# A four-layer graph network on one core: loading scalars and biases first, and choosing which degree sums block 0 leaves to layer 1

## The chip, the core and the metric

The kernel runs on one core of a Trainium2 chip. Its engines work side by side, each through its own queue in order: TensorE (PE: matmuls; its weight loads are shown as PEld), VectorE (DVE), ScalarE (ACT), GpSimd (POOL), and SyncE (SP), which here only issues loads and stores. The metric is device time in microseconds (us), lower is better; the median of several runs is given.

## What is computed

Four layers follow each other on 4096 nodes with 64 features and one dense 4096 x 4096 adjacency matrix `adj` (64 MiB in float32). Each layer normalizes x, applies a ReLU, mixes rows through `adj` in its own way, and adds the result to x:

```python
h = relu(layernorm(x)); x = x + relu((adj @ h) @ W0.T + b0)            # layer 0
h = relu(layernorm(x))                                                 # layer 1
#   h, q, k by "lorentz_linear" with scale, scale_q, scale_k
#   att = adj * sigmoid((2 + 2 * qm @ k.T) / att_scale + att_bias);  x += normalized(att @ h)
h = relu(layernorm(x))                                                 # layer 2
#   deg = adj.sum(axis=1); w = adj / deg; weights from distances; x += expmap(...)
h = relu(layernorm(x))                                                 # layer 3
#   ranks of the nonzero entries of each row; x += (mask * 2**-(k - pos)) @ (h @ W3) + b3
```

The row sums of `adj` (`deg`, the degrees) are needed in layer 2 only. They can be collected whenever a piece of `adj` is in the core's memory, in layer 0 or in layer 1.

## The kernel before

**Tiling.** The rows of the result are cut into 8 blocks of 512 (`NB`, index `ib`). For one block, `adj` is read transposed in 16 groups (`NG`, index `g`), each a tile of 128 partitions x 2 x 512 float32 (512 KB), by one load on SP's queue (`feed`, line 837). Layers 0, 1 and 3 read all 128 groups each; ten buffers hold the groups in the first two layers (two pools of 6 and 4), so a load needs the buffer of the group ten places earlier.

**Start.** SP loads x in four quarters (line 175) and then the groups. For each quarter, `before0` computes the layernorm: two VectorE operations, a square on ACT (`qT<-HL` in the profile), a sum and a scaling on VectorE, a power on GpSimd (`lo_n`), and a VectorE operation that writes `HA`, the operand of the matmuls. Four times this makes `HA` complete. Layer 0's groups are multiplied as soon as `HA`'s quarter and the group are there (`l0_sums`, tiles `acc<-adj,HA`).

**After a block of layer 0** its result goes through a tail of small steps (`after0`, `before1`): ACT copies the accumulator (`e`), VectorE folds the block's degree tile (`dg<-dg`, 128x512), PE makes four matmuls with `W0T` and four with the degree tile (`tr<-W0T,e`, `tr<-ones_f,dg`), VectorE copies `deg` and adds the bias and the residual (`h<-tr,lines`, `x<-h,x`), then the next layernorm, a transposition, a matmul with `W1T`, ACT's chain of small operations (a table load for the sigmoid among them), VectorE's `lo_n`, GpSimd's power, `HL`, its transposition, a matmul with `WqkT`, and so on to q and k.

**Degree sums.** `group` decides for every group in which layer it is added to the degree tile. Blocks 1 to 6 leave the groups of `LEFT` to layer 1, block 0 leaves those of `FRONT`, block 7 leaves none. So in block 0, twelve groups are summed on VectorE in layer 0 (`dg<-adj`, a copy, for the first, then `dg<-dg,adj`), and the four of `FRONT` in layer 1. A group that is summed keeps its buffer until both its matmul and its sum are done.

**Scalars and biases.** Five scalars and two biases (`b0`, `b3`) are loaded into one row `line` (1 x 133). A matmul with a row of ones spreads it over 128 partitions, and a copy from PSUM makes `lines`, from which `scal`, `b0` and `b3` are read. Before the change, these loads are the first seven of a list of fifteen that ACT issues in `constants`, one after another; the eight after them are weights (`W0T` twice, `W1T`, its bias, and the q and k weights and biases). The last group of block 0 may be multiplied only when `lines` is planned (`None if d["last"] and "lines" not in opened`).

**The order.** The program is written out by a planner, `in_turn`. It holds one generator per strand of work; each yields an engine and an earliest time, and the strand that can start first by the planner's own costs (class `Pace`) is recorded next. Each engine then executes in exactly that order. A changed cost or a changed strand early on therefore moves operations in all engines' orders for as long as the strands of layers 0 and 1 are mixed. The order is fixed when the program is built: on the chip an operation whose operand is late holds up everything behind it on its engine. While PE is planned to wait, `keep_warm` adds filler matmuls.

**DMA semaphores.** The loads of SP and ACT report their landing through eight semaphores, dealt out in turn over both queues in the program's order. A load whose semaphore is still in use by an earlier load waits for that one to land before it is issued, and holds up what is behind it in its queue.

In the profile nearly all operations show line 139, that of the recording helper, so they are told apart by their tiles.

Of the kernel before, what the change touches and what calls it, by code (L numbers as in the profile page):

```python
# [19 lines left out]
D = 64  # L20
# [6 lines left out]
NG = NC // G  # L27
HALVED = 2
LEFT = (3, 7, 11, 15)
FRONT = (4,5,6,7,)  # L30
LAST = 2
WAIT = 0.6
EARLY = 12
# [113 lines left out]
def kernel(ctx: ExitStack, tc: tile.TileContext, a: dict, out: bass.AP):  # L147
# [3 lines left out]
    nc = tc.nc  # L151
    pace = Pace()
    PE, DVE, ACT, POOL = (
        InOrder(tc, e, pace, name)
        for e, name in (
            (nc.tensor, "PE"), (nc.vector, "DVE"), (nc.scalar, "ACT"), (nc.gpsimd, "POOL"),
        )
    )
# [23 lines left out]
    def fetch(t, src, to=loads):  # L182
        to.append(lambda: ACT.dma_start(out=t, in_=src))
# [9 lines left out]
    NS = len(SCALARS)  # L193
    line = const.tile([1, NS + 2 * D], F32, name="line")
    for n, name in enumerate(SCALARS):
        fetch(line[:, n : n + 1], a[name])
    for n, name in enumerate(("b0", "b3")):
        fetch(line[:, NS + n * D : NS + (n + 1) * D], a[name].rearrange("d o -> o d"))
    ones_row = const.tile([1, P], F32, name="ones_row")
    DVE.memset(ones_row, 1.0)  # L200
    lines = const.tile([P, NS + 2 * D], F32, name="lines")
# [58 lines left out]
    def later_constants():  # L260


        def patterns():
            yield "POOL", lambda: 60.0
            for t, one in [(t, 1.0) for t in rbs] + [(t, 0.25) for t in lbs]:
                POOL.memset(t, 0.0)
                for k in (1, 3):
                    POOL.memset(t[:, :, k, 1:2], one)

        def weights_of_ranks():  # L270


            yield "DVE", lambda: 150.0
            near_f = st["rows"].tile([P, P], F32, name="near_f", bufs=1)
            make_lower_triangular(nc, near_f, val=-1.0, diag=False)
            for q in range(4):
                b = slice(q * Q, (q + 1) * Q)
                DVE.tensor_copy(far[b, :], near_f[b, b])
            diag_f = st["rows"].tile([P, P], F32, name="diag_f", bufs=1)
            DVE.tensor_scalar(diag_f, ident, HERE, None, ALU.mult)  # L280
            yield "DVE", lambda: 150.0
            DVE.tensor_add(near_f, near_f, diag_f)
            DVE.tensor_copy(near, near_f)


            yield "DVE", lambda: 150.0
            DVE.memset(pick, 0.0)
            DVE.memset(spread, 0.0)
            for k in range(KH):
                DVE.memset(pick[:, k, k : k + 1], 1.0)  # L290
            for r in range(4):
                yield "DVE", lambda: 150.0
                b = slice(r * Q, (r + 1) * Q)
                for h in range(2):
                    to = spread[b, h, :, h * NC // 2 : (h + 1) * NC // 2]
                    DVE.tensor_copy(
                        to.rearrange("p q (k r) -> p q k r", r=4)[:, :, :, r],
                        ident[b, r * Q : r * Q + KH].unsqueeze(1).to_broadcast([Q, 4, KH]),
                    )

        return patterns(), weights_of_ranks()
# [48 lines left out]
    spare = [0, 1]  # L350

    def bank():
        k = spare.pop(0)
        t = (ps_two if k else ps_tr).tile([P, W], F32, tag=f"tr{k}", name="tr")
        in_use.append((t, k))
        return t

    def emptied(t):
        k = [k for k in in_use if k[0] is t][0]
        in_use.remove(k)  # L360
        spare.append(k[1])
# [219 lines left out]
    def after0(ib, acc, st):  # L581
        e = rows.tile([P, W], F32, tag="e", name="e")
        ACT.copy(e, acc)
        st["acc_free"][ib % 2] = pace.latest
        yield ON_V, lambda: st["dg_done"].get((0, ib))
        dg = st["dg"][0, ib]
        DVE.tensor_add(dg[:, 0, :], dg[:, 0, :], dg[:, 1, :])
        yield TURN

        ps = bank()  # L590
        v, n = ps[:, 0 : CB * D].rearrange("p (c k) -> p c k", k=D), CB * D
        for c in range(CB):
            b = slice(c * P, (c + 1) * P)
            PE.matmul(v[:, c, :], e[:, b], W0T, start=True, stop=True)
            PE.matmul(ps[:, n + c : n + c + 1], dg[:, 0, b], ones_f, start=True, stop=True)
        st["dg_free"][ib % 2] = pace.latest
        yield ON_V
        DVE.tensor_copy(deg[:, cs(ib), :], ps[:, n : n + CB].unsqueeze(2))
        s = rt("h", [P, CB, D])
        DVE.tensor_add(s, v, b0.to_broadcast([P, CB, D]))  # L600
        DVE.scalar_tensor_tensor(
            x[:, cs(ib), :], s, 0.0, x[:, cs(ib), :], ALU.max, ALU.add
        )
        yield ON_V
# [121 lines left out]
    def follow(gen, on=ON_V, evicts=False):  # L726

        tail.append(
            {"gen": gen, "on": on, "at": pace.latest, "slot": None, "evicts": evicts, "need": None}
        )  # L730
# [24 lines left out]
    def latest(*times):  # L755
        return None if None in times else max(times)
# [56 lines left out]
    opened = {}  # L813

    def with_mark(layer, ib, *gens):
        for gen in gens:
            yield from gen
        rows_at[layer, ib] = pace.latest
# [21 lines left out]
    def used(d):  # L840
        d["left"], d["at"] = d["left"] - 1, max(d["at"], pace.latest)

    def ready(t, more=0.0):
        return pace.ready[pace.name(t)] + more

    def arrival(d, more=0.0):
        return ready(d["adj"], more) if "adj" in d else None
# [43 lines left out]
    def group(layer, ib, g):  # L891
        degree = (g in (LEFT if ib else FRONT) and ib < NB - 1) == (layer == 1)
        return {"layer": layer, "ib": ib, "g": g, "degree": degree, "left": 1 + degree, "at": 0.0}
# [3 lines left out]
    l0 = [group(0, ib, g) for ib in range(NB) for g in range(NG)]  # L897
    l1 = [group(1, ib, g) for ib in range(2) for g in range(BEHIND)]
# [5 lines left out]
    for d in l0 + l1:  # L904
        n = done[d["layer"], d["ib"]] = done.get((d["layer"], d["ib"]), 0) + 1
# [19 lines left out]
    def degree_sums(layer, work):  # L925

        dg = st["dg"]
        for d in work:
            if not d["degree"]:
                continue  # L930
            first = (layer, d["ib"]) not in dg
            yield "DVE", lambda: latest(
                arrival(d, 4.0), st["dg_free"][d["ib"] % 2] if first else 0.0
            )
            if first:
                t = w01.tile([P, G, W], F32, tag="dg", name="dg", bufs=2)
                dg[layer, d["ib"]] = t
                st["dg_free"][d["ib"] % 2] = None
                DVE.tensor_copy(t, d["adj"])
            else:  # L940
                t = dg[layer, d["ib"]]
                DVE.tensor_add(t, t, d["adj"])
            used(d)
            if d is [e for e in work if e["degree"] and e["ib"] == d["ib"]][-1]:
                st["dg_done"][layer, d["ib"]] = pace.latest
# [5 lines left out]
    def l0_sums():  # L951
        for d in l0:
# [6 lines left out]
            if d["last"]:  # L959
                ib = d["ib"]  # L960
                follow(with_mark(1, ib, after0(ib, acc, st), before1(ib, st)), ON_S, evicts=True)

    def constants():
        for k in range(len(loads)):
            yield "ACT", lambda: 18.0 + 0.5 * k
            loads.pop(0)()
        yield "PE", lambda: 28.0 if spare else None
        ps = bank()
        PE.matmul(ps[:, 0 : NS + 2 * D], ones_row, line, start=True, stop=True)
        yield "DVE", lambda: ready(ps)  # L970
        DVE.tensor_copy(lines, ps[:, 0 : NS + 2 * D])
        emptied(ps)
        opened["lines"] = pace.latest
        yield "ACT", lambda: 32.0

        ACT.activation(es, scal[:, 0:3], AF.Exp)

        DVE.reciprocal(att_a, scal[:, 4:5])
        DVE.tensor_scalar(att_a, att_a, 2.0, None, ALU.mult)
        DVE.tensor_add(att_b, att_a, scal[:, 3:4])  # L980
        for k in range(len(later_loads)):
            yield "ACT", lambda: 240.0 + 0.5 * k
            later_loads.pop(0)()
# [146 lines left out]
    def l2_clamps():  # L1130
        for d in work:
            yield "POOL", lambda: d.get("square")
            v = part(d, d["v"]) if not d["shared"] else d["v"].rearrange("p c i -> p (c i)")[:, CLAMPED:]
            POOL.tensor_scalar(v, v, FLOOR, None, ALU.max)
            d["clamped"] = pace.latest
# [390 lines left out]
    def l3_sum():  # L1526
# [33 lines left out]
            (l2_coshs(), 0, once), (l2_clamps_v(), -1, once), (l2_weights2(), 1, lambda d: 2 if d["two"] else 1 if d["first"] else 0),  # L1560
        ),
        l2_clamps(), l2_gathers(), l3_weights(), l3_pass(), l3_masks(), l3_bias(),
        degree_sums(0, l0), degree_sums(1, l1), constants(), *later_constants(),
    ])


# [43 lines left out]
```

## Time and profile before

| | |
|---|---|
| median of 3 runs | 1097.06 us (1095.85 to 1101.96) |
| the profiled execution | 1101.81 us, of which the profile's span is 1100.1 us |
| busy, share of the span | PE 95%, DVE 85%, ACT 72%, PEld 42%, POOL 24% |
| moved by DMA | 271.77 MB, mean 247 GB/s |

How to read it: the span runs from the first to the last instruction of the profiled execution. A timeline line gives start, length, engine, source line, operation, out<-in, shape and count, and in brackets the idle time of the engine just before it with what ended it. Lines of the same kind that follow closely are merged, and the length is that of all of them. [...] In a table by stage, the clock and the loads' rate stand at the end of each line.

### The profile page before, as it was taken

Reading aid. Unit: us, or ns where it says so; the run is one execution under the profiler, and the core shown is the slowest. Engines: PE = TensorE matmul, PEld = TensorE weight load, DVE = VectorE, ACT = ScalarE, POOL = GpSimd, SP = SyncE. Lnnn points to the kernel's source line nnn. Section 1 sums busy time; section 2 is a strip of 40 time slices with the busy share of each in tenths; the row PEclk is TensorE's granted clock in tenths of the full one; section 3 lists DMA queues with packets and bytes.
Section 4 is the critical chain, followed back from the end, with each engine's and each line's share of the span. In section 5 each row is a group of like instructions: output and inputs, shape, how many; then the busy total and the mean of one; then the engine's idle time right before and its main releaser. Section 6 shows DMA issues by size and latency. Waiting matters only on the chain.

```text
span 1100.1 us, 16913 instructions
## 1 busy us (share of the span) xinstructions
PE 1043.9 (95%) x6030; PEld 466.8 (42%) x6030; DVE 931.7 (85%) x1526; ACT 788.1 (72%) x1224; POOL 261.0 (24%) x151
## 2 busy tenths in 40 slices
PE   7899999899999999999999999999999988999998
PEld 3344444333233333354544444445454443444444
DVE  7678999888999999888989998989899998666551
ACT  1144545476777777799989879888898866677776
POOL 3022312110110011243334334344444420000000
PEclk9989999999999999999999999999999998999999
DMA  8999999866687777544543543544545539899950
GB/s 309 406 346 389 381 389 382 306 227 217 212 277 265 241 262 271 177 143 167 192 173 125 192 181 118 190 151 155 171 156 189 190 128 398 346 409 408 411 225 10
DMA packets 76202, 271.77 MB, mean 247 GB/s; under 512 B 9046, under 2 KB 10070, under 8 KB 76118
## 3 DMA queue, kind: packets, MB, share of 16 engines
q1 hardware_dynamic: 75456, 270.57, 67.3%
q8 instruction: 47, 0.77, 0.3%
q14 instruction: 37, 0.30, 0.1%
q10 hardware_dynamic: 662, 0.13, 0.1%
HBM read 269.62 MB, written 1.05 MB: 246 GB/s over the span
## 4 chain that ended last, share of the span: by engine, by line
PE 54%; DVE 22%; issue 7%; ACT 6%; POOL 5%; DMA 3%; SPq 0%; ACTq 0%; POOLq 0%; DVEq 0%
PE acc L139 27%; PE mm L139 17%; PE tr L139 10%; DVE dg L139 5%; POOL v L139 5%; DVE t L139 3%; DVE w L139 3%; DVE sig L139 3%; DMA adj<-in_adjT_dram 3%; ACT sig L139 2%; ACT t L139 1%; ACT v L139 1%; DVE x L139 1%; DVE h L139 1%; ACT lo_sq L139 1%
## 5 line engine op out<-in xcount | busy, mean ns | idle before, releaser
L139 PE MATMUL acc<-w,HA 128*65 128x256 f32 (+1 forms) x736 | 246.2, 469 | 9.1 <-DVE w L139 8.9
L139 POOL TENSOR_SCALAR v<-v 128x1024 f32<-128x1024 f32 (+1 forms) x72 | 173.0, 2402 | 251.6 <-ACT v L139 248.9
L139 ACT ACTIVATE sig<-mm,att_b,att_a 128x1024 f32<-128x1024 f32 x128 | 150.8, 1203 | 58.0 <-PE mm L139 54.0
L139 ACT ACTIVATE wt<-mm,down 128x1024 fp32r<-128x1024 f32 x128 | 136.1, 1111 | 47.1 <-PE mm L139 44.7
L139 DVE TENSOR_TENSOR sig<-sig,adj 128x1024 f32<-128x1024 f32 x128 | 152.6, 1220 | 12.3 <-ACT sig L139 12.1
L139 DVE TENSOR_TENSOR dg<-dg,adj 128x1024 f32<-128x1024 f32 x113 | 137.9, 1221 | 1.6
L139 PE MATMUL mm<-qT,kT 64*64 64x512 f32 (+1 forms) x896 | 130.2, 599 | 6.6 <-ACT sig L139 6.1
L139 PEld LDWEIGHTS acc<-w,HA 128*65 128x65 f32 x736 | 94.3, 138 | 92.5 <-issue 50.2
L139 PE MATMUL acc<-sig,HL 64*64 64x512 f32 (+1 forms) x896 | 131.7, 603 | 1.4 <-DVE sig L139 1.4
L139 PE MATMUL acc<-adj,HA 128*64 128x512 f32 x512 | 125.6, 624 | 5.7 <-DMA adj<-in_adjT_dram 5.6
L139 ACT ACTIVATE v<-v,minus 128x1024 f32<-128x1024 f32 x72 | 79.1, 1098 | 27.5 <-POOL v L139 26.1
L139 DVE SCALAR_TENSOR_TENSOR t<-mm,t 128x1024 f32<-128x1024 f32 x72 | 83.6, 1160 | 14.9 <-PE mm L139 11.0
L139 DVE SCALAR_TENSOR_TENSOR t<-t,v 128x1024 f32<-128x1024 f32 x72 | 83.3, 1157 | 3.5 <-ACT t L139 2.9
L139 DVE TENSOR_TENSOR w<-t,adj 128x1024 f32<-128x1024 f32 x72 | 83.6, 1161 | 1.4
L139 DVE TENSOR_TENSOR w<-tr,adj 128x512 f32<-128x512 f32 x120 | 77.5, 683 | 7.4 <-PE tr L139 7.2
L139 ACT ACTIVATE t<-t 128x1024 f32<-128x1024 f32 x72 | 72.2, 1003 | 14.1 <-DVE t L139 14.0
L139 ACT ACTIVATE v<-mm 128x1024 f32<-128x1024 f32 x72 | 69.6, 967 | 13.7 <-PE mm L139 13.7
L139 PE MATMUL mm<-RT,LT 64*128 64x512 f32 (+1 forms) x288 | 78.0, 618 | 0.0
L139 PE MATMUL acc<-wt,S 128*128 128x512 f32 x256 | 76.2, 424 | 0.6 <-ACT wt L139 0.4
L139 ACT ACTIVATE t<-v 128x1024 f32<-128x1024 f32 x72 | 72.7, 1010 | 2.1
L139 ACT ACTIVATE v<-v 128x1024 f32<-128x1024 f32 x72 | 72.1, 1002 | 0.0
L139 PEld LDWEIGHTS mm<-qT,kT 64*64 64x64 f32 (+1 forms) x896 | 37.8, 140 | 77.9 <-ACT sig L139 35.4
(217 smaller groups left out, 1380.2 us busy)
## 6 DMA issues: line engine op xcount, KB each, us to landing
adj<-in_adjT_dram SPq DMA_DIRECT2D x512, 512.0 KB, 5.1
x<-in_x_dram SPq DMA_DIRECT2D x4, 256.0 KB, 4.1
out_dram<-h SPq DMA_DIRECT2D x8, 128.0 KB, 2.0
W<-in_W_dram ACTq DMA_DIRECT2D x3, 16.0 KB, 4.0
line<-in_b_dram ACTq DMA_DIRECT2D x2, 0.2 KB
W0T<-in_W0T_dram ACTq DMA_DIRECT2D x2, 16.0 KB
line<-in_scale_dram ACTq DMA_DIRECT2D x1, 0.0 KB
line<-in_scale_q_dram ACTq DMA_DIRECT2D x1, 0.0 KB
```

The lines of the kernel that those rows point to most:

```text
L139: done = self.tc.keep_in_program_order(getattr(self.engine, op)(*args, **kw))
```

## The change

Seven loads leave the list of `constants` and are issued from ACT's queue where `line` is declared, ahead of everything that ACT does. The matmul that spreads `line` and the copy to `lines` become a strand of their own, `spread_lines`: the matmul is wanted from 10 us of the planner's time on instead of 28, and the copy is made by ACT instead of VectorE. `FRONT` names groups 0 to 3 instead of 4 to 7.

```diff
-FRONT = (4,5,6,7,)
+FRONT = (0, 1, 2, 3)
...
     for n, name in enumerate(SCALARS):
-        fetch(line[:, n : n + 1], a[name])
+        nc.scalar.dma_start(out=line[:, n : n + 1], in_=a[name])
     for n, name in enumerate(("b0", "b3")):
-        fetch(line[:, NS + n * D : NS + (n + 1) * D], a[name].rearrange("d o -> o d"))
+        nc.scalar.dma_start(out=line[:, NS + n * D : NS + (n + 1) * D], in_=a[name].rearrange("d o -> o d"))
...
+    def spread_lines():
+        yield "PE", lambda: 10.0 if spare else None
+        ps = bank()
+        PE.matmul(ps[:, 0 : NS + 2 * D], ones_row, line, start=True, stop=True)
+        yield "ACT", lambda: ready(ps)
+        ACT.copy(lines, ps[:, 0 : NS + 2 * D])
+        emptied(ps)
+        opened["lines"] = pace.latest
+
     def constants():
         for k in range(len(loads)):
             yield "ACT", lambda: 18.0 + 0.5 * k
             loads.pop(0)()
-        yield "PE", lambda: 28.0 if spare else None
-        ps = bank()
-        PE.matmul(ps[:, 0 : NS + 2 * D], ones_row, line, start=True, stop=True)
-        yield "DVE", lambda: ready(ps)
-        DVE.tensor_copy(lines, ps[:, 0 : NS + 2 * D])
-        emptied(ps)
-        opened["lines"] = pace.latest
         yield "ACT", lambda: 32.0
...
-        degree_sums(0, l0), degree_sums(1, l1), constants(), *later_constants(),
+        degree_sums(0, l0), degree_sums(1, l1), spread_lines(), constants(), *later_constants(),
```

What else moves is the planner's doing. Around the first block's end the orders of PE and VectorE become:

| engine | before | after |
|---|---|---|
| PE | 15 groups, the matmul of `line`, 5 groups, degree matmuls of block 0 | 2 groups, the matmul of `line`, 16 groups, degree matmuls of block 0 |
| PE | 7 groups, `h`, 1 group, `W1T`, 6 groups, `HL`, 1 group, `WqkT`, degree matmuls of block 1 | 7 groups, `h`, 1 group, `W1T`, 5 groups, `HL`, 1 group, `WqkT`, 2 groups, degree matmuls of block 1 |
| VectorE | third `HA`, copy and 2 sums, fourth `HA`, 5 sums, `lines`, 3 sums, `att`, 1 sum, fold, copy, 2 sums, `deg` | third and fourth `HA`, copy and 10 sums, `att`, 1 sum, fold, copy, `deg` |

## The prediction, on record before the changed kernel ran

> **What bounds the kernel now.** I read the page's forty slices first, then busy time by stage, then the timelines of VectorE (DVE), the waits of SyncE's queue, and the chain of waits over the first 90 us. By stage (columns: stretch, its length, then busy us and instruction counts of PE, PEld, DVE, ACT, POOL, then the granted TensorE clock, the DMA share, GB/s):
>
> ```profile
> 20.00:40.00 20.00, 15.00 (x55) 3.95 (x51) 14.56 (x18) 0.69 (x2) 0.00 (x0) 0.83 0.94 360
> 40.00:60.00 20.00, 16.99 (x85) 6.08 (x85) 16.21 (x24) 5.86 (x18) 5.60 (x12) 1.00 1.01 397
> 60.00:80.00 20.00, 20.00 (x90) 10.61 (x88) 15.75 (x24) 8.31 (x35) 2.80 (x5) 0.75 0.88 332
> 150.00:180.00 30.00, 28.99 (x161) 13.37 (x159) 29.18 (x67) 15.37 (x67) 5.71 (x4) 1.00 1.00 388
> 215.00:262.00 47.00, 45.82 (x206) 15.50 (x202) 35.42 (x46) 30.66 (x41) 5.44 (x3) 0.98 0.71 243
> ```
>
> Layer 0 (to about 215 us) is held by two things that are nearly equal: the adjacency loads (388 to 397 GB/s; the best single microseconds show about 410, so a 524,288-byte group takes 1.28 us) and VectorE (97% at 150 to 180). From 215 us PE is the bound. Anything won in the first 40 us reaches the end only if PE and VectorE keep it through layer 0; then all later work starts that much sooner. The two places that the change touches, in VectorE's timeline:
>
> ```profile
> 21.54 6.25 DVE L139 TENSOR_TENSOR dg<-dg,adj 128x1024 f32<-128x1024 f32 x5
> 32.89 0.30 DVE L139 COPY lines<-tr 128x133 f32<-128x133 f32 x1 [5.10 <-PE tr L139]
> ...
> 38.46 0.69 DVE L139 TENSOR_TENSOR dg<-dg 128x512 f32<-128x512 f32 x1
> ...
> 42.20 0.15 DVE L139 COPY deg<-tr 128x4 f32<-128x4 f32 x1
> ...
> 66.25 0.16 DVE L139 COPY deg<-tr 128x4 f32<-128x4 f32 x1 [2.48 <-PE tr L139]
> ```
>
> VectorE stands still for 5.10 us because `lines` waits for a PE matmul that is queued behind 15 groups. The chain of waits around it (start, length, what) shows the second trouble, in the loads:
>
> ```profile
> 16.30 3.02 DMA line<-in_scale_q_dram
> ...
> 20.54 3.80 DMA W1T<-in_W1T_dram
> ...
> 24.40 4.41 DMA adj<-in_adjT_dram
> ```
>
> An adjacency load leaves at 24.40, just after a weight load has landed. The built program says why: all DMAs of SP and ACT take eight completion semaphores in turn, and each DMA waits until the earlier one on its semaphore has landed. The 15 small loads that ACT issues from 15.75 on take six of the eight. PE's waits for data show the price: groups 9 to 13 can start at 19.36, 22.09, 23.80, 25.93 and 28.85, so four groups took 9.5 us where 4 x 1.28 = 5.1 would do: 4.4 us of loading lost.
>
> **The change, part by part.**
>
> *Seven tiny loads move to ACT's front.* By the waits of the built program, x's fourth quarter now waits on SP for the first tiny load, and the first adjacency load behind it for x's second quarter. x's first quarter lands at 4.37 (0.79 + 3.58), the second by 262,144 bytes at 410 GB/s later, about 5.0. So the first adjacency load, and with it every later one in SP's queue, is issued at about 5.1 instead of 2.63. Its data queued behind x before; what is lost lies between 0 and 2.4 us, and I take 0.8, since x's own 1 MB occupies the queue until about 6.4 either way. PE needs the group only at 11.16. On ACT the sixth tiny load waits for x's first quarter, and the table load (1.28) follows: 4.37 + 2 x 0.25 + 1.28 = 6.2, where the first square ran at 5.84. That shifts VectorE's opening chain by 0.4 us (0 to 1.3). For a tiny load in a quiet queue the trace has no row; 3.02 us is the nearest, in a full queue. [...]
>
> *From 15 us.* The loads of groups 10 and 11 still wait, on their semaphores, for the landings of groups 8 and 9 (about 1.2 us of emptiness remains), but ACT's eight weight loads go out from about 16 us instead of 19.33, so the adjacency loads behind them find their semaphores free. Group 13 lands at 28.85 - 4.4 + 0.8 + 1.2, about 26.4: **2.4 us earlier**.
>
> *Groups 0 to 3 lose their degree sums in layer 0.* Before, their buffers came free behind VectorE (the first copy ended at 18.50); now behind PE (about 12 to 15 us). The count of sums is the same, 12 in block 0. VectorE: the fourth `HA` at 19.39 + 0.4, done 20.5; one copy 0.69, ten sums of 1.24, three `att` operations 0.45, one sum, the fold 0.65: 35.95, against 39.1. **3.1 us earlier.** The data is no limit: group 15 lands near 29. The copy of `lines` costs ACT 0.2 to 0.4 us (its `es` 0.21, its 128x256 copy 0.37) between two squares, where it was idle for 2.87 us; without that cover it would cost VectorE's opening chain as much. Its PE matmul (0.71) sits behind two groups at about 13.5, where PE has data in hand.
>
> *What takes this back.* The changed order puts 18 groups, not 20, ahead of block 0's degree matmuls, and one VectorE operation (the copy), not three, between the fold and `deg`. PE would be done with group 17 at about 32.5 (26.4 + 4 x 1.28 + 0.93) and wait 3.4 us for the fold. In this trace such waits are followed by half clock; first a wait of 1.95 us in PE's timeline, then the ten microseconds after it (columns as in the first table):
>
> ```profile
> 58.93 0.60 PE L139 MATMUL tr<-ident,HL 128*64 128x128 f32 x4 [1.95 <-DVE HL L139]
> ```
>
> ```profile
> 60.00:70.00 10.00, 10.00 (x38) 6.42 (x36) 7.28 (x14) 5.16 (x25) 0.34 (x4) 0.50 0.91 348
> ```
>
> At half clock the eight degree matmuls took 3.3 us (62.80 to 66.14), at full clock 1.9 (39.03 to 40.98). So `deg` comes at about 39.4 instead of 42.20, yet VectorE has done two sums less (2 x 1.22) by then and idles 2.7 us. In block 1 the same happens: `HL` is transposed at about 57.2 (58.93 before), after 5 instead of 6 groups behind the W1T matmuls and so after 2.6 us of idle PE; with half clock again the second `deg` lands near 66.0, against 66.25. What is kept by then lies between 0.3 us (both stretches at half clock) and 3.1 us (neither). I take 1.0, nearer the low end, since 1.95 us of idleness was enough here.
>
> The Trainium skill, page "TensorE: Matmul & The Clock Gate", Part 1, says that the clock halves after an idle window of about 3.4 us. By that rule alone the 1.95 us wait above would have cost nothing, and block 1's 2.6 us would not either; by it `deg` of block 1 would come about 2.5 us sooner. The row speaks against the rule here, and I go by the row.
>
> *Later order.* The order is planned as a whole, so layers 0 and 1 are interleaved differently to about 470 us; layer 3 and the later part of layer 2 stand as before. PE's extra filler matmuls (five) cost 1.4 us at most by its 0.27 us transposes, and stand in waits. I count this as 0, with 3 us to either side.
>
> **Sum.** The profiled execution took 1101.81 us (span 1100.1), 4.75 above the median of 1097.06, inside the runs shown; the difference is what I carry over: 1097.06 - 1.0 = **1096.0**, 1093 to 1100 by the bounds of this case alone.
>
> **Rivals.**
> - *The gain is kept.* PE stays warm in blocks 0 and 1. Then 3.1 us stay, and the loading hole at 60 to 80 us (332 against 397 GB/s: 65 x 20 / 410 = 3.2 us) closes: 1097.06 - 6.3 = 1090.8. For it: 5.10 us of idleness really go. Against: PE waits longer for the fold than before.
> - *The removed stall was free.* While VectorE stood still, loads ran on: 28 to 33 us show 356 to 426 GB/s. If the loads alone set the pace and the 0.8 and 1.2 us above are larger, nothing moves: 1097.1.
> - *Slower: buffers held in layer 1.* The four sums that layer 1 owes block 0 are now those of its first four groups, loaded some 8 x 1.28 = 10 us earlier, while VectorE is full (29.18 of 30 us) and, in the changed order, still makes the sums after its fourth `sig` product. Four of ten buffers are then held back while layer 0's last loads pass at 165 to 200 us. If they are held for more than about 5 us, four loads come late: 4 x 1.28 = 5.1 us, with nothing kept of the head: 1102.2.
>
> **Chances.** Forecast (about 1096) 0.48, free stall (1097) 0.12, gain kept (1091) 0.21, buffers held (1102) 0.19. A measurement of this kernel can tell about 0.5% (5.5 us) from no change: faster 0.21, same 0.60, slower 0.19. The range, 1088 to 1103, takes in both rivals and the 3 us of the reordering.
>
> **What would show it.** Right: no idle VectorE at 28 to 33 us; group 13 by 26 to 27 us; fold near 36; PE idle before it, a clock of 0.5 after it; `deg` of block 1 within 2 us of 66. Wrong: a full clock through 70 us and a second `deg` before 64 (gain kept); SP waiting at 165 to 200 us for `dg` sums more than before, and loads under 330 GB/s there (buffers held); first `HA` later than 11.5 (the front costs more than I took).

## The result, and the profile after

| | median | range of runs | against before |
|---|---|---|---|
| before | 1098.37 us | 1095.85 to 1101.96 (6) | |
| after | 1107.95 us | 1104.60 to 1109.95 (6) | 1.0067, 95% interval 1.0047 to 1.0086 |

The change costs 0.67%, some 7.4 us, where 1096.0 (1088 to 1103) was forecast. The ratio compares the runs of both kernels and is not the quotient of the two medians, which is 1.0087 here (9.6 us), just above the interval. The profiled execution of after took 1104.60 us (span 1102.9), the lowest of its runs; that of before, 1101.81, was near the top of its own. The two traces therefore show 2.8 us of the 7.4, and what follows uses them for where time goes, and the ratios for how much.

By stage, the changed kernel in the five stretches that were shown of before (same columns):

```profile
20.00:40.00 20.00, 14.34 (x66) 4.61 (x66) 18.30 (x23) 0.69 (x2) 0.00 (x0) 1.00 0.96 371
40.00:60.00 20.00, 17.38 (x90) 6.90 (x87) 15.37 (x21) 9.03 (x32) 2.92 (x2) 1.00 1.03 407
60.00:80.00 20.00, 18.33 (x96) 7.63 (x95) 17.79 (x29) 7.86 (x30) 7.43 (x15) 1.00 0.95 352
150.00:180.00 30.00, 29.64 (x156) 12.75 (x154) 29.24 (x67) 18.15 (x70) 9.83 (x5) 1.00 0.92 361
215.00:262.00 47.00, 43.28 (x210) 15.92 (x208) 35.45 (x48) 29.13 (x39) 4.50 (x3) 1.00 0.74 257
```

VectorE is busy for 18.30 of the 20 us in which it was busy for 14.56, and the clock is 1.00 in all five stretches (0.83 and 0.75 before in the first and the third). The head is better. The last line shows the other side: PE, the bound there, works 43.28 of 47 us (45.82 before). VectorE's timeline of the changed kernel at the places shown of before:

```profile
20.88 12.56 DVE L139 TENSOR_TENSOR dg<-dg,adj 128x1024 f32<-128x1024 f32 x10
...
35.07 0.69 DVE L139 TENSOR_TENSOR dg<-dg 128x512 f32<-128x512 f32 x1
...
37.58 0.16 DVE L139 COPY deg<-tr 128x4 f32<-128x4 f32 x1 [1.21 <-PE tr L139]
...
60.63 0.16 DVE L139 COPY deg<-tr 128x4 f32<-128x4 f32 x1 [1.64 <-PE tr L139]
```

Ten sums run without a gap, the 5.10 us stall is gone, and `deg` of the first two blocks comes 4.6 and 5.6 us earlier. This lead is 5.8 us at block 3 (104.2 for 110.0 us), 0.8 at block 6, and at block 7 it is a lag of 5.8 (219.9 for 214.1). Layer 1 brings the two level (0.4 us apart at the end of its first block) and ends 1.1 us early; layer 2 begins 1.2 us late (its first `t<-mm,t`) and is 3.6 us late from the sixth on. So the gain is made, and lost in three places: the first two use up most of the lead, the third makes the lag. In VectorE's timeline, the first:

```profile
128.93 0.17 DVE L139 TENSOR_SCALAR lo_n<-lo_n 128x8 f32<-128x8 f32 x1 [2.34 <-ACT lo_sq L139]
...
129.46 0.69 DVE L139 TENSOR_TENSOR dg<-dg 128x512 f32<-128x512 f32 x1
```

The fold of block 4 stands behind the `lo_n` of another block's tail, which is not ready, and VectorE waits for it. Adding up all its waits over 0.25 us between the `deg`s of blocks 3 and 6 gives 6.15 us, against 2.79 before: 3.4 of the 5.0 us lost in this stretch are waits for small steps. VectorE also makes two degree sums more there (34 for 32). The second place, after and then before:

```profile
211.44 3.71 DVE L139 TENSOR_TENSOR sig<-sig,adj 128x1024 f32<-128x1024 f32 x3
...
216.32 0.69 DVE L139 TENSOR_TENSOR dg<-dg 128x512 f32<-128x512 f32 x1
216.93 2.35 DVE L139 TENSOR_TENSOR sig<-sig,adj 128x1024 f32<-128x1024 f32 x2
219.93 0.16 DVE L139 COPY deg<-tr 128x4 f32<-128x4 f32 x1 [0.65 <-PE tr L139]
```

```profile
210.55 0.68 DVE L139 TENSOR_TENSOR dg<-dg 128x512 f32<-128x512 f32 x1
...
214.08 0.15 DVE L139 COPY deg<-tr 128x4 f32<-128x4 f32 x1
```

VectorE is nearly full in both: between the `deg`s of blocks 6 and 7 it is busy for 45.9 of 48.2 us, before for 40.7 of 41.6. It has made 16 of layer 1's products by block 7's `deg` (12 before): 4 x 1.22 = 4.9 us of work done ahead, which is most of the 6.7 us that the stretch is longer. The work done ahead is not lost by itself: by 240 us 24 products are made, where before had 21. But the last two groups of layer 1's first blocks need block 7's q and k. PE's timeline, after and then before:

```profile
247.99 1.08 PE L139 MATMUL acc<-sig,HL 128*64 128x512 f32 x4 [0.58 <-DVE sig L139]
250.37 0.66 PE L139 MATMUL tr<-ident,qq 128*128 128x128 f32 x4 [1.31 <-ACT qq L139]
...
251.98 1.99 PE L139 MATMUL mm<-qT,kT 64*128 64x512 f32 x8 [0.73 <-ACT kT L139]
```

```profile
247.01 0.66 PE L139 MATMUL tr<-ident,qq 128*128 128x128 f32 x4
247.59 1.99 PE L139 MATMUL mm<-qT,kT 64*128 64x512 f32 x8
```

Before, `qq` is transposed between other matmuls without a wait; after, PE runs out of other work and stands for it. The third place is where layer 2 begins, in VectorE's timeline after and before:

```profile
470.82 1.23 DVE L139 SCALAR_TENSOR_TENSOR t<-mm,t 128x1024 f32<-128x1024 f32 x1 [1.89 <-ACT t L139]
...
480.44 0.42 DVE L139 TENSOR_REDUCE r_n<-r_sq 128x4 f32<-128x252 f32 x1 [1.88 <-ACT r_sq L139]
```

```profile
469.58 1.23 DVE L139 SCALAR_TENSOR_TENSOR t<-mm,t 128x1024 f32<-128x1024 f32 x1
...
477.07 0.41 DVE L139 TENSOR_REDUCE r_n<-r_sq 128x4 f32<-128x252 f32 x1
```

VectorE waits for ACT in both places. The first time ACT's `t` stands behind the copy `LT`, which waits 1.07 us for PE. The second time the cast `RB`, the copies `lb` and a `v` that waits for GpSimd stand ahead of `r_sq` (480.01; 476.46 before, where they come after it). From the end of layer 1 to layer 2's ninth `t<-mm,t` the changed kernel loses 4.8 us.

### The profile page after: what moved, and what is told of

Same layout as the page of the kernel before. It is cut to its first block, busy times and chain, and to the rows that moved or that the text cites. A ratio compares the mean times of both kernels' runs of the same rounds, so it can differ in the third digit from the quotient of the medians.

```text
span 1102.9 us, 16918 instructions
## 1 busy us (share of the span) xinstructions
PE 1041.2 (94%) x6040; PEld 464.1 (42%) x6040; DVE 932.8 (85%) x1525; ACT 788.7 (72%) x1225; POOL 261.8 (24%) x151
## 4 chain that ended last, share of the span: by engine, by line
PE 47%; DVE 26%; issue 8%; ACT 7%; POOL 6%; DMA 5%; SPq 0%; ACTq 0%; DVEq 0%; POOLq 0%
PE acc L139 24%; PE mm L139 14%; PE tr L139 10%; DVE sig L139 6%; DVE dg L139 5%; POOL v L139 5%; DMA adj<-in_adjT_dram 4%; DVE t L139 3%; DVE w L139 3%; ACT t L139 1%; ACT sig L139 1%; ACT v L139 1%; DVE h L139 1%; POOL lo_s L139 1%; DVE r_n L139 1%
## 5 line engine op out<-in xcount | busy, mean ns | idle before, releaser
L139 PE MATMUL acc<-w,HA 128*65 128x256 f32 (+1 forms) x736 | 246.1, 469 | 10.8 <-DVE w L139 10.7
L139 POOL TENSOR_SCALAR v<-v 128x1024 f32<-128x1024 f32 (+1 forms) x72 | 173.3, 2406 | 256.1 <-ACT v L139 253.5
L139 ACT ACTIVATE sig<-mm,att_b,att_a 128x1024 f32<-128x1024 f32 x128 | 150.5, 1202 | 50.0 <-PE mm L139 45.9
L139 ACT ACTIVATE wt<-mm,down 128x1024 fp32r<-128x1024 f32 x128 | 135.9, 1110 | 45.8 <-PE mm L139 43.4
L139 DVE TENSOR_TENSOR sig<-sig,adj 128x1024 f32<-128x1024 f32 x128 | 152.6, 1220 | 9.4 <-ACT sig L139 7.0
L139 DVE TENSOR_TENSOR dg<-dg,adj 128x1024 f32<-128x1024 f32 x113 | 137.9, 1221 | 1.7
L139 PE MATMUL mm<-qT,kT 64*64 64x512 f32 (+1 forms) x896 | 130.5, 600 | 7.3 <-ACT sig L139 6.5
L139 PEld LDWEIGHTS acc<-w,HA 128*65 128x65 f32 x736 | 94.2, 138 | 94.4 <-issue 50.3
L139 PE MATMUL acc<-adj,HA 128*64 128x512 f32 x512 | 124.1, 609 | 9.2 <-DMA adj<-in_adjT_dram 9.0
L139 PE MATMUL acc<-sig,HL 64*64 64x512 f32 (+1 forms) x896 | 129.9, 600 | 2.0 <-DVE sig L139 1.8
L139 ACT ACTIVATE v<-v,minus 128x1024 f32<-128x1024 f32 x72 | 79.1, 1098 | 26.4 <-POOL v L139 24.9
L139 DVE SCALAR_TENSOR_TENSOR t<-mm,t 128x1024 f32<-128x1024 f32 x72 | 83.5, 1160 | 15.1 <-PE mm L139 11.0
L139 DVE SCALAR_TENSOR_TENSOR t<-t,v 128x1024 f32<-128x1024 f32 x72 | 83.3, 1157 | 3.7 <-ACT t L139 3.7
L139 DVE TENSOR_TENSOR w<-t,adj 128x1024 f32<-128x1024 f32 x72 | 83.5, 1160 | 1.4
L139 ACT ACTIVATE t<-t 128x1024 f32<-128x1024 f32 x72 | 72.2, 1003 | 16.9 <-DVE t L139 16.9
L139 DVE TENSOR_TENSOR w<-tr,adj 128x512 f32<-128x512 f32 x120 | 77.5, 683 | 7.4 <-PE tr L139 7.3
L139 PE MATMUL mm<-RT,LT 64*128 64x512 f32 (+1 forms) x288 | 78.2, 619 | 1.5 <-DVE t L139 1.4
L139 ACT ACTIVATE v<-mm 128x1024 f32<-128x1024 f32 x72 | 69.5, 966 | 13.8 <-PE mm L139 13.8
L139 PE MATMUL acc<-wt,S 128*128 128x512 f32 x256 | 75.6, 421 | 0.5 <-ACT wt L139 0.3
L139 ACT ACTIVATE t<-v 128x1024 f32<-128x1024 f32 x72 | 72.7, 1010 | 2.1
L139 ACT ACTIVATE v<-v 128x1024 f32<-128x1024 f32 x72 | 72.1, 1001 | 0.0
L139 PEld LDWEIGHTS mm<-qT,kT 64*64 64x64 f32 (+1 forms) x896 | 37.6, 140 | 79.3 <-issue 39.0
```

What stands on the lines that cost most here:

```text
L139: done = self.tc.keep_in_program_order(getattr(self.engine, op)(*args, **kw))
```

## The experiments

Theory (order): the head gains 5 to 7 us, and the plan that follows from the new times loses more. Rivals: buffers (groups 0 to 3 of layer 1 keep their buffers until late sums), and head (the loads in front cost more than they save).

To tell them apart the order has to be held fixed. Seven of the kernels (3, 4, 5, 7, 8, 11, 12) take the planner's choices from a list: `ORDER` names, for every step, the strand that a planner took next, and the number of filler matmuls ahead of it. The step is the first name in it whose strand is ready. The condition says from where on (here from the end of block 0 in layer 0; in 8 and 12 from the start). The traces bear it out: from block 2 of layer 0 on, VectorE goes through the same operations in kernel 5 as before, one for one. Recording stands 30 lines lower in these kernels (L169 for L139).

```diff
+            step = None
+            if pace.now >= 46.0:
+                step = next((s for s in plan if s[0] in can), None)
+                best = can[step[0]]
             pace.now, what = best
```

All ratios are to runs of the kernel before made beside them, medians 1099.5 to 1100.9 us.

**1. The loads and the copy alone.** The change with one line undone:

```diff
-FRONT = (0, 1, 2, 3)
+FRONT = (4, 5, 6, 7)
```

> The seven loads and the ACT copy as in the changed kernel, FRONT as before (groups 4 to 7). Its planned order is close to that of the changed kernel (PE differs in 10 places). Order theory (the loss lies in the order that the planner makes once the head is earlier): about 7 us over the kernel before, like the changed kernel, 4 to 9. Buffer theory (layer 1 holds the buffers of block 0's groups 0 to 3, which this kernel does not do): the head's gain stays, 3 to 6 us under the kernel before. Head theory (the loads in front cost more than they save): about 7 us over, with a later deg of block 0 in the profile; the order theory wants deg of block 0 near 37.6 us, as in the changed kernel.

Measured 1102.54, ratio 1.0028 (1.0007 to 1.0049). `deg` of block 0 comes at 36.5 us, so the head theory falls. The time lies between what order and buffers expected: slower, but less than the whole change.

**2. FRONT alone**, with loads and copy as before:

```diff
-FRONT = (4,5,6,7,)
+FRONT = (0, 1, 2, 3)
```

> FRONT (0, 1, 2, 3) alone, loads and the copy of lines as before. Buffer theory: 4 to 8 us over the kernel before. Order theory: it says nothing of the size, since the planner makes a third order; the profile must show any difference at the end of layer 0 or between layers 1 and 2, 0 to 8 us over, and the 5 us stall of VectorE near 28 us is still there. Head theory: within 2 us of the kernel before.

Measured 1105.13, ratio 1.0045 (1.0025 to 1.0066); VectorE's stall is there (5.13 us at 34.57). `deg` of block 6 is 2.5 us early, that of block 7 is 4.3 late. Buffers and order both allow it.

**3. The whole change in the order of before** (`ORDER` of before from 46 us on).

> The whole change, and the changed kernel's own order up to 46 us of the planner's time (end of block 0 in layer 0); from there on every engine executes in the order of the kernel before. Order theory: the head's gain of 4.6 us at block 0's deg reaches the end, 3 to 6 us under the kernel before (about 1094), 10 to 13 under the changed kernel. Buffer theory and head theory: about as slow as the changed kernel, 5 to 8 us over the kernel before, since groups 0 to 3 still owe their sums to layer 1 and the loads still stand in front.

Measured 1109.21, ratio 1.0090 (1.0062 to 1.0119): the order theory's number is missed, with the sign wrong. But the trace does not show a costly head either: `deg` is 7.4 us early from block 2 to block 6, and then 7.1 us late at block 7. VectorE's timeline:

```profile
186.40 0.69 DVE L169 COPY dg<-adj 128x1024 f32<-128x1024 f32 x1
...
191.95 1.23 DVE L169 TENSOR_TENSOR dg<-dg,adj 128x1024 f32<-128x1024 f32 x1 [2.26 <-DMA adj<-in_adjT_dram]
...
195.55 1.23 DVE L169 TENSOR_TENSOR sig<-sig,adj 128x1024 f32<-128x1024 f32 x1 [1.24 <-DMA adj<-in_adjT_dram]
...
203.35 2.36 DVE L169 TENSOR_TENSOR sig<-sig,adj 128x1024 f32<-128x1024 f32 x2 [5.28 <-ACT sig L169]
```

Group 0's product was made at 165.96, but its degree sum, which frees its buffer, only at 186.40, where before had that of group 4. Loads come late, VectorE waits for them, and 14.5 us go between two `deg`s. This is the buffer rival, in an order made for other groups.

**4. The kernel before in the changed order** (from 46 us on, nothing else of the change).

> The kernel before without the change (loads, copy and FRONT as before), but from 46 us of the planner's time on every engine executes in the changed kernel's order. Order theory: slower than the kernel before by 6 to 13 us, since it has the changed order's loss and not the head's gain; layer 2 starts at least 4 us later than in the kernel before. Buffer theory and head theory: within 2 us of the kernel before.

Measured 1112.79, ratio 1.0118 (1.0091 to 1.0146); layer 2 starts 6.6 us late. The changed order is costly without the changed head, as the order theory says. How much of this comes from forcing an order on a head that it was not planned for is not shown.

**5. Loads and copy, FRONT as before, in the order of before.** Kernel 1 with `ORDER` of before from 46 us on; against kernel 3 only FRONT differs.

> As the run with the new head and the order of before, but with FRONT as before (groups 4 to 7): the loads in front and the copy by ACT are all that is left of the change, and every engine keeps the order of the kernel before from 46 us of the planner's time on. Buffer theory (groups 0 to 3 of layer 1 hold four of ten buffers until their late sums; this cost 14.5 us between the degs of blocks 6 and 7 in that run): no such loss, deg of block 7 at least 4 us earlier than before, and 4 to 7 us under the kernel before. Theory that an earlier head is lost at the end of layer 0 whatever FRONT is (PE and VectorE bound there, or block 7's tail): within 2 us of the kernel before or over it, and deg of block 7 not earlier.

Measured **1092.43, ratio 0.9926 (0.9902 to 0.9949)**, faster than both kernels. `deg` of block 7 comes 6.4 us early, and 6.5 us are there at every later mark of layers 0 and 1. The stretch from 60 to 80 us of this kernel loads at 408 GB/s (332 before), and that from 215 to 262 keeps PE at 46.84 us:

```profile
60.00:80.00 20.00, 19.22 (x107) 8.88 (x106) 18.25 (x31) 11.83 (x44) 4.53 (x3) 1.00 1.03 408
...
215.00:262.00 47.00, 46.84 (x238) 16.96 (x242) 38.74 (x51) 31.53 (x44) 5.44 (x3) 1.00 0.72 240
```

Kernels 1 and 5 do the same work with the same head; the order from block 0's end on is 1.0028 against 0.9926, **1.0% or 11 us**.

**6. Layer 1's sums listed first.** The planner gives ties to the strand listed first, and VectorE is full, so layer 1's sums came last (the first at 188.4 us in the changed kernel).

```diff
-        degree_sums(0, l0), degree_sums(1, l1), spread_lines(), constants(), *later_constants(),
+        degree_sums(1, l1), degree_sums(0, l0), spread_lines(), constants(), *later_constants(),
```

> The whole change, but the strand of layer 1's degree sums is listed ahead of that of layer 0's, so that the planner, which gives ties to the strand listed first, makes block 0's four sums in layer 1 as soon as VectorE is free. Buffer theory: the buffers of groups 0 to 3 come free some 8 us sooner, loading at 170 to 190 us returns from 282 and 245 to over 320 GB/s, deg of block 7 comes no later than before (214), and since this order joins that of the kernel before in the middle of layer 1, the time is 1 to 6 us under the kernel before. Rival (the late sums are not what holds the loads): still 5 to 9 us over, loading under 300 GB/s there.

Measured 1102.72, ratio 1.0032 (1.0012 to 1.0052): missed. The first sum of layer 1 moves from 188.4 to 181.3 us, but of the lead only 0.3 us is left at block 3 already, `deg` of block 7 is 7.7 us late, and 180 to 190 us load at 177 GB/s. A new plan lost the gain somewhere else, and the time, 3.5 us over, fits neither expectation; loading under 300 GB/s is what the rival expected.

**7. The changed order until layer 1's 41st sum, then that of before.**

> The changed kernel with its own order until its 41st group of layer 1 is summed, and the order of the kernel before from there on. Theory of two losses (about 6 us at the end of layer 0, which layer 1 gives back, and 4 us between layers 1 and 2 by the changed order): the second loss goes, 2 to 5 us over the kernel before and 3 to 5 under the changed kernel; the first products of layer 2 no later than before by more than 1 us. Rival (layer 2 starts late because of what layers 0 and 1 left behind, not by its own order): as the changed kernel, 6 to 9 us over.

Measured 1103.35, ratio 1.0051 (1.0028 to 1.0074), between the two expectations. From the end of layer 1 to layer 2's ninth `t<-mm,t` it loses 1.6 us, where the changed kernel loses 4.8: two thirds of the third loss go with the order. But it ends layer 1 1.0 us late, the changed kernel 1.1 early, so at the ninth the two are only 1.0 us apart (2.6 and 3.6 late). The other traces agree on this place: kernels 4, 8 and 9, which execute the changed order there, lose 4.8 us each, and kernels 3, 5, 11 and 12, in the order of before, at most 0.1.

**8. One more buffer in the changed order.**

```diff
-    adj01 = early.enter_context(tc.tile_pool(name="adj01", bufs=4))
+    adj01 = early.enter_context(tc.tile_pool(name="adj01", bufs=5))
-    adj_pools.append((adj01, 4, []))
+    adj_pools.append((adj01, 5, []))
```

> The changed kernel in exactly its own order on every engine, with one more buffer for the adjacency groups of layers 0 and 1 (eleven for ten). Buffer theory: the hole in loading at 171 to 183 us shrinks, deg of block 7 comes 1 to 4 us sooner than in the changed kernel; of that little reaches the end, since layer 1 gave the loss back already and the loss between layers 1 and 2 stays: 3 to 7 us over the kernel before. Rival (the buffers are not what holds the loads): deg of block 7 at 219 to 221 us as in the changed kernel, 6 to 8 us over.

Measured 1109.50, ratio 1.0081 (1.0053 to 1.0108); `deg` of block 7 at 219.5 (219.9). As the rival expected, one more buffer in the changed kernel's own order does not bring block 7 forward. But the holes in loading are there in both (263 GB/s from 170 to 190 us in the changed kernel, 272 and 256 in the two halves of that stretch here, 382 before), so what closing them would bring is not shown. VectorE has other work listed and is busy through them (19.48 of the 20 us in the changed kernel, 19.70 before).

**9 and 10. The kernel before, planned from a slightly different number.** Nothing of the change is in these two.

```diff
-        self.free.update(DMA=5.2, ANY=0.0)
+        self.free.update(DMA=5.5, ANY=0.0)
```

> The kernel before with nothing of the change; only the planner's start value for the first adjacency load is 5.5 instead of 5.2 us. The work is the same, the planned order is another one (from layer 1 on close to that of the changed kernel). Theory that the changed kernel's loss is a matter of which plan the planner falls into: 4 to 9 us over the kernel before, with layer 2 starting 3 us or more late. Rival (the loss comes from what the change itself does): within 2 us of the kernel before.

```diff
-        yield "PE", lambda: 28.0 if spare else None
+        yield "PE", lambda: 27.0 if spare else None
```

> The kernel before; only the planner's wanted time of the matmul that spreads line is 27 instead of 28 us. A second draw of the same kind, with yet another order. Plan theory: 2 to 8 us over the kernel before. Rival: within 2 us.

Measured 1110.59, ratio 1.0085 (1.0052 to 1.0117), and 1106.92, ratio 1.0065 (1.0043 to 1.0087). Two nudges of the planner cost as much as the change does. From 205 us on, VectorE and ACT go through the changed kernel's order in the first: 16 products ahead of block 7's `deg`, waits of 1.89 and 1.88 us at 469.64 and 479.26, layer 2 late by 2.5 us. The plan of before is the best of the freely planned ones run here.

**11. The whole change in the order of before, with layer 1's first four sums moved right behind the products of the same groups.**

> As the run with the whole change and the order of before (which lost 14.5 us between the degs of blocks 6 and 7), but with the first four sums of layer 1 moved right behind the four sig products of the same groups in VectorE's order, so that the buffers of groups 0 to 3 are held for one sum and not for 10 to 15 us. Buffer theory: the loss at the end of layer 0 goes (deg of block 7 at 206 to 210 us), 4 to 7 us under the kernel before, as with FRONT 4 to 7. Rival (groups 0 to 3 are costly there for another reason, such as more VectorE work ahead of block 7's tail): deg of block 7 after 215 us, 4 to 10 us over.

Measured 1098.53, ratio 0.9990 (0.9974 to 1.0005). Against kernel 3 the moved sums give back 1.0%, 11 us, so the late sums, which held the buffers, were most of its loss of 18 (kernel 3 against 5), and VectorE no longer waits for loads there. `deg` of block 7 is 0.6 us early (213.5), not the 4 to 8 that were expected, probably because four sums of VectorE now stand ahead of block 7's steps. With FRONT 0 to 3 some 7 us more are spent than with 4 to 7 (kernel 5) even so.

**12. The loads alone, every engine in the order of before**; matmul and copy of `line` where they were.

> Only the seven loads go in front; matmul and copy of line (on VectorE) and every engine's order stay exactly as before. If the gain of the head comes from the loads (semaphores found free, four groups in 5 to 7 us instead of 9.5): VectorE's 5.1 us stall shrinks to about 2, deg of block 0 at 39 to 41 us, 2 to 5 us under the kernel before. If it comes from the matmul and the copy being early: the stall stays over 4 us and the time is within 1.5 us of the kernel before.

Measured 1096.45, ratio 0.9968 (0.9951 to 0.9985). VectorE's timeline:

```profile
33.99 0.30 DVE L169 COPY lines<-tr 128x133 f32<-128x133 f32 x1 [5.63 <-PE tr L169]
...
43.29 0.16 DVE L169 COPY deg<-tr 128x4 f32<-128x4 f32 x1
```

The stall is as long as before and `deg` of block 0 is 1.1 us later, so the lead at the first block needs the early matmul and copy; the loads alone do not give it. The 3.5 us by which this kernel is faster anyway appear later: 1.4 at block 2, behind a clock of 0.83 where before's execution had 0.50, and 1.7 more between block 7's `deg` and the end of layer 1's first block, where before's clock shows 0.83 (210 to 220 us) and this one's 1.00. Over all runs the clock accounts for them: at a mean granted clock of 0.989 to 0.991, eight runs of this kernel average 1096.5 us and ten of the kernel before 1096.8. Its runs have 0.990 on average, those of before beside it 0.987; whether the loads are the reason is not shown.

## Why the prediction was wrong

**The step that failed** is *Later order*: "I count this as 0, with 3 us to either side". It measured 11 us (kernels 1 and 5), with 6.5 and 8.5 us from nudges that change nothing else (10 and 9). The account of the 7.4 us: the head gives 0.74%, the new plan takes 1.02%, and FRONT takes 0.39% more (after against kernel 1), in us -8.1, +11.2 and +4.3. So FRONT is a second term that the sum had at nothing, as a rival alone, and the head a third, -1.0, that was too small. In the place of the 0 the runs showed 3.4 us of waits for small steps behind block 3, four products made ahead of block 7's tail, and 4.8 us lost where layer 2 begins.

A rival to these figures is the granted clock, and it has a share in them. The 70 runs of the kernel before made beside the experiments average 1102.0 us at a mean clock of 0.979 to 0.985, 1096.8 at 0.989 to 0.991, and 1095.6 at 0.992 to 0.994. All six runs of kernel 5 lie in the last class, with 1092.0, and three of kernel 1, with 1100.3. At the same clock the head is thus worth some 3.5 us, and the order costs 8.3: the order stays the largest term, and over half of the 8.1 goes with a higher clock. Part of that clock can be the head's own doing (PE waits 0.42 us for `HL` of block 0 in kernel 5, 1.95 before); how much is not shown.

Point by point:

- *Loads in front*: right. The first group's load leaves at 5.11 us (5.1), the first square runs at 5.97 (6.2). x's fourth quarter leaves at 2.16 us, as before: if it waits for the first tiny load, issued at 0.78, that load landed within 1.4 us, less than half of the 3.02 of the nearest row.
- *Group 13 2.4 us earlier*: wrong. PE starts groups 9 to 13 at 20.53, 22.69, 25.57, 27.32 and 28.51 us, so the last is 0.3 us earlier: the four after group 9 take 8.0 us instead of 9.5, but group 9 itself is 1.2 us later. ACT's weight loads still hold semaphores: the chain of waits goes from `W0T` over the k weights to a group issued at 25.12:

```profile
15.88 4.83 DMA W0T<-in_W0T_dram
...
20.73 4.31 DMA WqkT<-in_WkT_dram
...
25.12 9.40 DMA adj<-in_adjT_dram
```

- *VectorE's 3.1 us*: right in size (the fold ends at 35.76; 35.95 said), with the cause named, the stall of 5.10 us.
- *What takes this back*: wrong. Because the groups came later than I had them, PE was not early: it ends group 17 at 35.64 and has no wait ahead of the degree matmuls. Nor did block 1's wait (1.88 us) halve the clock. `deg` came at 37.58 and 60.63, not 39.4 and 66.0; 5.6 us were kept, not 1.0. Of the bounds 0.3 to 3.1 I took the low end from a single row, and the high end was exceeded.
- *Gain kept* (1090.8): what it says of the head is right, and kernel 5 shows it at 1092.43, without the change of FRONT and with the order held still: full clock and 408 GB/s from 60 to 80 us, as the rival had it.
- *Free stall* (1097.1): wrong, since kernel 5 is 0.7% faster (3.5 us at the same clock).
- *Buffers held* (1102.2): the right side, and the mechanism exists. It costs up to 18 us in an order not made for it (kernel 3 against 5), more than the 5.1 priced. In the changed kernel itself its sign came half: from 165 to 200 us the loads run at 306 GB/s (360 before; under 330 was asked), but SP does not wait longer for degree sums (21.5 us, 24.1 before), and an eleventh buffer gains nothing. Whether FRONT's 4.3 us there come from held buffers or from the order that it leads to is not shown, so the right side was in part luck.

I had weighed the new order only around the ends of the first two blocks. Its later part can be read in advance as well: 16 products for 12 ahead of block 7's `deg`, and `lo_n` ahead of a fold, both stand in VectorE's order.

## What to carry to other kernels

A greedy planner makes every early change a redraw of all that follows. Where such a planner writes the order, measure its scatter first (two nudges of a number that should not matter), and try a change in the old order as well as in the new one: here the same loads and the same copy are 0.7% faster in one and 0.3% slower in the other. A gain at the head is worth what the order behind it keeps, and a buffer that waits for a low-priority reader belongs into the price of moving that reader.

## What was not expected of the hardware

Waits of PE of one kind (for `HL` of block 0) had different ends. In the kernel with the loads and the copy alone (PE's timeline, then the stretch behind it):

```profile
53.06 0.60 PE L139 MATMUL tr<-ident,HL 128*64 128x128 f32 x4 [1.82 <-DVE HL L139]
```

```profile
55.00:60.00 5.00, 5.00 (x16) 2.48 (x16) 2.83 (x4) 3.38 (x14) 0.00 (x0) 0.50 1.03 407
```

1.82 us there and 1.95 before were followed by a clock of 0.50. After 1.88 us (changed kernel), 1.84 (8), 2.10 (2), 2.13 (7) and 3.05 us (9) it stayed at 1.00; after 2.13 us (6) and 2.46 us (12) it was at half for a part of the stretch behind the wait (means of 0.69 and 0.83), after 3.85 us (4) for nearly all of it (0.52). So the length of a wait of 2 to 3 us does not tell whether the clock falls, and one execution's half clock is no term for a forecast. What does tell in these ten traces is where the wait lies: the clock changes only on a grid of 3.41 us, which starts at another point in each execution. It fell where at least 1.82 us of the wait lay in one step of the grid (1.82 in kernel 1, 1.95 before, 2.13 in 6, 2.27 in 12, 2.37 in 4) and stayed where the wait was cut by the grid into parts of at most 1.79 us (1.28 in the changed kernel, 1.42 in 2, 1.54 in 9, 1.70 in 8, 1.79 in 7). This is a reading of ten rows: in the whole traces no step with over 1.9 us of idle PE kept the full clock, but some with less lost it. The Trainium skill, page "TensorE: Matmul & The Clock Gate", Part 1, calls the activity window of about 3.4 us free-running, so that the point of a transition depends on where in the window the first matmul falls; the grid and the mixed outcomes agree with that, and the two falls after waits of less than 2 us are sooner than its idle window of 3.4 us.

At half clock the matmuls do not take twice as long: in the trace of before a 128x512 product of layer 0 takes 1.06 us at 0.50 and 0.59 at 1.00 (medians), one of the `W0T` matmuls 0.42 and 0.28.

A hole in loading need not leave VectorE idle: the changed kernel loads at 263 GB/s from 170 to 190 us (382 before), and VectorE is busy for 19.48 of the 20 us.
